# Moving the pass for far sampling points of a fused attention, deformable-convolution and MLP kernel into the main schedule, with its tables in DRAM

## The chip, the cores and the metric

The kernel runs on one core of one Trainium2 chip. The metric is the device time of one execution in microseconds, as the median of several runs. A trace of one profiled execution of the kernel before is at hand as well.

## The reference, cut to what matters

Four images of 64 x 64 tokens with 256 channels pass through self-attention over the 4096 tokens of an image (queries and keys of 32 channels, a residual scaled by a learned factor). Then comes a block of three parts: LayerNorm; a deformable 3 x 3 convolution (DCNv3) with residual; LayerNorm, an MLP (256 to 1024 to 256, GELU) and residual. All is float32.

The change concerns the deformable convolution. Per token, a small branch computes 16 groups x 9 points = 144 sampling points, each with an offset in x, an offset in y and a softmax weight:

```python
px = loc_x * Win - 0.5            # token + point of the 3x3 grid + offset
py = loc_y * Hin - 0.5
x0 = jnp.floor(px); y0 = jnp.floor(py)
lx = px - x0;       ly = py - y0
val = gather(y0, x0) * ((1 - ly) * (1 - lx))[..., None] + gather(y0, x0 + 1) * ((1 - ly) * lx)[..., None] \
    + gather(y0 + 1, x0) * (ly * (1 - lx))[..., None] + gather(y0 + 1, x0 + 1) * (ly * lx)[..., None]
out = jnp.einsum('nhwgpc,nhwgp->nhwgc', val, mask).reshape(N, H, W, C)
```
`gather` reads the 16 channels of the point's group from the projected image, zero outside the padded image. The sampled sum is then multiplied with a 256 x 256 output matrix.

## The kernel before, in words

**Tiling.** The 16384 tokens are cut into 64 units (4 images x 16, `NU` = 16 per image) of 256 tokens: four image rows, two tokens on each of the 128 partitions. For each unit there are stages, written as dictionaries of small named steps:

- `project` and attention, for the next image's keys and for this unit's tokens; attention is most of TensorE's work.
- `front`: residual, first LayerNorm, input projection, whose result goes to the DRAM image `xp`.
- `plan`: the depthwise branch, the heads that give offsets and mask (tile `om`, 2 x 432 numbers per partition, stored to DRAM as `omd` in `weigh`, L676), the bilinear weights as `hat`, and from those the weights `wn` of a 5 x 5 window.
- `sample`: VectorE multiplies five shifted rows `win` with `wn` (`times`, L785) and adds them up (`plus`, L793; `across`); the sums go to DRAM as `spd`.
- `back`: output projection, second LayerNorm and MLP, through `finish` (L818 to 901); its last step `end` (L885) adds the MLP's result `pmlp` to `x1b`, and SyncE stores it to the output (L912).

**Order.** `whole()` collects the steps of all units, gives each the time `slot * T + WHEN[stage][step]` (T = 60, table `WHEN`), sorts them and emits them in that order, under a manual schedule for TensorE, VectorE, ScalarE and GpSimd. A unit with number s has attention in slot s, `front` in s + 1, `plan` in s + 2, `sample` and `back` in s + 3. Plain DMAs are issued by SyncE's queue in an order of the framework's own.

**Far points.** The 5 x 5 window holds every point whose offsets lie within 1. For others, `am` = min(1 − |x|, 1 − |y|) (`nearer`, L642) is negative; their weight is set to zero (`near`, L681), and `count` (L654 to 661) adds up their number per partition and unit in `cnt`. So the sum in `spd` lacks them, and the tokens after attention, to which the convolution's result is added, are kept in DRAM as `x1d`.

**After the last unit.** The main program calls `whole(False)` (L955). Then:

1. A test over all attention sums and mask sums (L957 to 975), whose last steps are `plow` on TensorE (L970) and three small VectorE operations (L972 to 975). A loop with 0 or 1 rounds (L976) does everything again in a general form, `whole(True)`, if a value is out of range.
2. Tables of indices, ten of them, made by GpSimd's iota (L994) and a VectorE cast (L996), one after the other through one buffer.
3. `cnt` is added up (L1015), the largest over partitions found (L1017 to 1021), and loaded as the number of rounds (L1022).
4. The loop of rounds (L1042 to 1161). A round takes one far point on every partition: it picks the last unit with one (L1045 to 1053), gathers the whole row of `omd` (indirect DMA on GpSimd, L1025), recomputes `am`, finds the point, and picks its x, y, mask, group and row with one-hot multiplies and sums (L1083, L1084). Then it gathers the four corner pixels (`s_px`), adds them to the token's gathered row of `spd`, runs `finish(x1, sp, "fx", 1)` for that one token per partition, and scatters the result to the output (L1030).

Of the kernel before, what the change touches and what calls it, by code (L numbers as in the profile page):

```python
# [8 lines left out]
F32 = mybir.dt.float32  # L9
# [7 lines left out]
def tile_attention_dcnv3_block(  # L17
# [21 lines left out]
    nc = tc.nc  # L39
# [68 lines left out]
    raw = const.tile([P, C // P, 2, CQ], F32, name="raw_qk")  # L108
# [80 lines left out]
    omd = dram.tile([B * NU * P, 2 * NOM], F32, name="omd")  # L189
    x1d_ = x1d.rearrange("(u q p) c -> u p q c", q=2, p=P)  # L190
    spd_ = spd.rearrange("(u q p) c -> u p q c", q=2, p=P)
    omd_ = omd.rearrange("(u p) m -> u p m", p=P)

# [68 lines left out]
    def transposed(src, name, n=2, pool=None, tag="m"):  # L262

        pt = (pool or ps).tile([P, C // P, 256], F32, tag=tag, name=f"pt_{name}")
        for k in range(C // P):
# [59 lines left out]
            "narrowed0": 84.81, "narrowed1": 89.91, "end": 93.7,  # L325
        },
# [224 lines left out]
    def plan(b, u, wns, general):  # L551
# [89 lines left out]
        def nearer():  # L641
            st["am"] = am = p1.tile([P, 2, S], F32, tag="am", name=f"am_{n}")  # L642
            nc.vector.tensor_tensor(
                am, st["hat"][:, 1, :, 0, :], st["hat"][:, 1, :, 1, :], ALU.min
            )

# [269 lines left out]

    def whole(general):
# [29 lines left out]
        if not general:  # L947
            steps += [(3.5 * i - 55.0, len(steps) + i, fn) for i, fn in enumerate(loads)]
# [5 lines left out]
    whole(False)  # L954
# [5 lines left out]
    safe = p1.tile([P, B * NU * 2], F32, tag="am", name="safe")  # L960
    flat = rall.rearrange("p u i -> p (u i)")
    nc.vector.tensor_scalar(safe, flat, 1e9, None, ALU.is_le)
    nc.vector.scalar_tensor_tensor(safe, flat, 1e-15, safe, ALU.is_ge, ALU.mult)
    for t, op, bound in ((least, ALU.is_ge, 1e-15), (most_, ALU.is_le, 1e15)):
        t = t.rearrange("p i g -> p (i g)")
        nc.vector.scalar_tensor_tensor(safe[:, : 2 * G], t, bound, safe[:, : 2 * G], op, ALU.mult)
    low = gx.tile([P, 1], F32, name="low")
    nc.vector.tensor_reduce(low, safe, AX.X, ALU.min)
    plow = ps.tile([1, P], F32, tag="m", name="plow")
    nc.tensor.matmul(plow, lhsT=low, rhs=ident, start=True, stop=True)  # L970
    again = gx.tile([1, 1], F32, name="again")
    nc.vector.tensor_reduce(again, plow, AX.X, ALU.min)  # L972
    nc.vector.tensor_scalar(again, again, -1.0, 1.0, ALU.mult, ALU.add)
    again_i = gx.tile([1, 1], I32, name="again_i")
    nc.vector.tensor_copy(again_i, again)
    with tc.For_i(0, nc.values_load(again_i[0:1, 0:1], min_val=0, max_val=1), 1):  # L976
        whole(True)
    main.close()


    fx = ctx.enter_context(tc.tile_pool(name="fx", bufs=1))
    UN = B * NU
    FAR = float(4 * max(H, W))
    BIG = 4096.0

    def table(shape, pattern, base, name, halves=False, step=0, cm=0):

        size = 1
        for d in shape:
            size *= d  # L990
        ti = fx.tile([P, size], I32, tag="ti", name=f"{name}_i")
        for r in range(2 if halves else 1):
            rows = slice(r * W, (r + 1) * W) if halves else slice(0, P)
            nc.gpsimd.iota(ti[rows], pattern=pattern, base=base + r * step, channel_multiplier=cm)  # L994
        tf = fx.tile([P, size], F32, name=name)
        nc.vector.tensor_copy(tf, ti)  # L996
        return tf

    part = table([1], [[0, 1]], 0, "part", cm=1)
    uid1 = table([UN], [[1, UN]], 1, "uid1")  # L1000
    h0 = table([UN], [[0, B], [4, NU]], 0, "h0")
    rb = table([UN], [[H + 4, B], [0, NU]], 0, "rb")
    sid1 = table([2 * S], [[1, 2 * S]], 1, "sid1")
    gid = table([2 * S], [[0, 2 * KP], [1, G]], 0, "gid")
    iid = table([2 * S], [[1, 2], [0, S]], 0, "iid")
    g16 = table([G], [[1, G]], 0, "g16")

    bx = table([2, 3, 3 * G], [[0, 2], [1, 3], [0, 3 * G]], -1, "bx", halves=True, cm=1)
    by = table([6, 3, G], [[0, 6], [1, 3], [0, G]], -1, "by", halves=True, step=1)
    nc.vector.tensor_scalar(by[:, S:], by[:, S:], 2.0, None, ALU.add)  # L1010

    ptr = fx.tile([P, 1], F32, name="ptr")
    nc.vector.memset(ptr, BIG)
    tot = fx.tile([P, 1], F32, name="tot")
    nc.vector.tensor_reduce(tot, cnt, AX.X, ALU.add)  # L1015
    ptot = ps.tile([1, P], F32, tag="m", name="ptot")
    nc.tensor.matmul(ptot, lhsT=tot, rhs=ident, start=True, stop=True)  # L1017
    most = fx.tile([1, 1], F32, name="most")
    nc.vector.tensor_reduce(most, ptot, AX.X, ALU.max)
    most_i = fx.tile([1, 1], I32, name="most_i")  # L1020
    nc.vector.tensor_copy(most_i, most)
    rounds = nc.values_load(most_i[0:1, 0:1], min_val=0, max_val=UN * 2 * S)  # L1022

    def gather(dst, src, idx):
        nc.gpsimd.indirect_dma_start(  # L1025
            out=dst, out_offset=None, in_=src, in_offset=bass.IndirectOffsetOnAxis(ap=idx, axis=0)
        )

    def scatter(dst, idx, src):
        nc.gpsimd.indirect_dma_start(  # L1030
            out=dst, out_offset=bass.IndirectOffsetOnAxis(ap=idx, axis=0), in_=src, in_offset=None
        )

    def integer(src, name, n=1):
        t = fx.tile([P, n], I32, tag=f"int_{name}", name=f"int_{name}")
        nc.vector.tensor_copy(t, src)
        return t

    def small(name, n=1):
        return fx.tile([P, n], F32, tag=f"s_{name}", name=f"s_{name}")  # L1040

    with tc.For_i(0, rounds, 1):  # L1042

        cu = small("cu", UN)
        nc.vector.scalar_tensor_tensor(cu, cnt, 0.0, uid1, ALU.is_gt, ALU.mult)  # L1045
        u1 = small("u1")
        nc.vector.tensor_reduce(u1, cu, AX.X, ALU.max)
        sel = small("sel", UN)
        nc.vector.tensor_scalar(sel, uid1, u1, None, ALU.is_equal)
        uu = small("uu")  # L1050
        nc.vector.tensor_scalar(uu, u1, 1.0, 0.0, ALU.subtract, ALU.max)
        at_om = small("at_om")
        nc.vector.scalar_tensor_tensor(at_om, uu, float(P), part, ALU.mult, ALU.add)
        om = fx.tile([P, 2 * NOM], F32, tag="f_om", name="f_om")
        gather(om, omd, integer(at_om, "om"))
        om = om.rearrange("p (i m) -> p i m", i=2)


        av = fx.tile([P, 2, 2 * S], F32, tag="f_av", name="f_av")
        ab = fx.tile([P, 2, 2 * S], F32, tag="f_ab", name="f_ab")  # L1060
        nc.vector.tensor_scalar(av, om[:, :, : 2 * S], -1.0, 0.0, ALU.mult, ALU.max)
        nc.vector.tensor_scalar(ab, om[:, :, : 2 * S], 0.0, None, ALU.max)
        nc.vector.scalar_tensor_tensor(  # L1063
            av, av, 1.0, ab, ALU.subtract, ALU.subtract, reverse0=True
        )
        am = fx.tile([P, 2, S], F32, tag="f_am", name="f_am")
        nc.vector.tensor_tensor(am, av[:, :, :S], av[:, :, S:], ALU.min)  # L1067
        am = am.rearrange("p i s -> p (i s)")
        nc.vector.scalar_tensor_tensor(am, am, 0.0, sid1, ALU.is_lt, ALU.mult)
        nc.vector.scalar_tensor_tensor(am, am, ptr, am, ALU.is_lt, ALU.mult)  # L1070
        s1 = small("s1")
        nc.vector.tensor_reduce(s1, am, AX.X, ALU.max)
        oh = fx.tile([P, 2 * S], F32, tag="f_oh", name="f_oh")
        nc.vector.tensor_scalar(oh, sid1, s1, None, ALU.is_equal)

        def pick(src, mask, dst, three=None):
            t = fx.tile([P, 2 * S], F32, tag="f_pick", name="f_pick")
            n = mask.shape[1]
            tv, mv = t[:, :n], mask
            if three:  # L1080
                tv = tv.rearrange("p (i s) -> p i s", i=2)
                mv = mask.rearrange("p (i s) -> p i s", i=2)
            nc.vector.tensor_mul(tv, src, mv)  # L1083
            nc.vector.tensor_reduce(dst, t[:, :n], AX.X, ALU.add)  # L1084

        xy, m, g, ti, rbs, h0s = small("xy", 2), small("m"), small("g"), small("ti"), small("rbs"), small("h0s")
        at = fx.tile([P, 2, S], F32, tag="f_at", name="f_at")
        nc.vector.tensor_add(at, om[:, :, :S], bx.rearrange("p (i s) -> p i s", i=2))
        pick(at, oh, xy[:, 0:1], True)
        at = fx.tile([P, 2, S], F32, tag="f_at", name="f_at2")  # L1090
        nc.vector.tensor_add(at, om[:, :, S : 2 * S], by.rearrange("p (i s) -> p i s", i=2))
        pick(at, oh, xy[:, 1:2], True)
        pick(om[:, :, 2 * S :], oh, m, True)
        nc.vector.scalar_tensor_tensor(m, u1, 0.0, m, ALU.is_gt, ALU.mult)
# [99 lines left out]
```

## Time and profile before

| what | us |
|---|---|
| median of 3 runs | 3935.21 (3930.83 to 3937.36) |
| the profiled execution | 3932.3 |
| its span in the trace | 3930.1 |
| TensorE busy in the span | 3788.7 (96%) |
| VectorE busy | 3418.2 (87%) |
| ScalarE busy | 1995.8 (51%) |
| GpSimd busy | 310.8 (8%) |
| mean granted TensorE clock | 0.981 of full |

The page shows TensorE (PE) nearly always busy: attention's `acc` matmuls alone (L471) are 1902.1 us. VectorE (DVE) is second; its largest groups are the window multiplies (L785, 936.6 us) and adds (L793, 759.0 us), of 1481 and 1482 ns each.

How to read the views: in the page's slices each digit is the busy share of a fortieth of the span (98 us), in tenths, and PEclk the clock granted to TensorE. A row of a timeline has the start, the duration, the engine, the line of the kernel, the operation with the tile it writes and those it reads, its shape, and in brackets the idle time of that engine ahead of it with what ended it. A row of a group of one line has min/median/max ns and the first and last start. `PEldq`, `DVEq`, `SPq` and so on are instructions of an engine's own sequencer, such as branches and DMA issues.

### The profile page before, as it was taken

What the parts mean: (1) busy time and instruction counts of PE and PEld (TensorE: products, weight loads), DVE (VectorE), ACT (ScalarE), POOL (GpSimd) and SP (SyncE); (2) the same over time, 40 slices, a digit from 0 to 9 for tenths busy, and PEclk for the clock granted to TensorE, in tenths of its full rate; (3) what the DMA queues carried; (4) which work ended last, traced back from release to release, by engine and by line L of the source; (5) the groups of instructions that cost most, each with busy time, mean ns of one, the idle gap of its engine ahead of it and who ended that gap; (6) DMA issues with size and microseconds to landing.
All of it is one profiled execution on the core that took longest, in us unless ns stands there. A gap on an engine that the chain in (4) does not pass through costs nothing. (4 is left out here: it accounts for less than half of the span.)

```text
span 3930.1 us, 56100 instructions
## 1 busy us (share of the span) xinstructions
PE 3788.7 (96%) x20284; PEld 3124.9 (80%) x20284; DVE 3418.2 (87%) x6160; ACT 1995.8 (51%) x3986; POOL 310.8 (8%) x437
## 2 busy tenths in 40 slices
PE   8999999999999999999999999999999999999853
PEld 7878888888888888888888888888888888888642
DVE  1499899999999999999989999999999999999992
ACT  4555555545555555555555554555555555555321
POOL 1000000000000000000000000000000000000001
PEclk9999999999999999999999999999999999999966
DMA  5334334335344333434443433433543334333320
GB/s 146 97 104 112 92 103 116 92 100 159 99 119 115 97 103 107 105 98 136 123 111 104 116 92 100 115 101 99 150 106 102 100 102 104 91 99 94 97 58 15
DMA packets 342769, 410.64 MB, mean 104 GB/s; under 512 B 136017, under 2 KB 292753, under 8 KB 342481
## 3 DMA queue, kind: packets, MB, share of 16 engines
q1 hardware_dynamic: 332544, 399.84, 38.2%
q10 hardware_dynamic: 8512, 3.43, 0.4%
q8 instruction: 162, 2.65, 0.3%
q0 software_dynamic: 1424, 3.69, 0.3%
q14 instruction: 127, 1.03, 0.1%
HBM read 277.00 MB, written 129.83 MB: 104 GB/s over the span
## 5 line engine op out<-in xcount | busy, mean ns | idle before, releaser
L471 PE MATMUL acc<-V,ex 128*128 128x257 f32 x8192 | 1902.1, 382 | 0.2 <-DVE x L500 0.2
L471 PEld LDWEIGHTS acc<-V,ex 128*128 128x128 f32 x8192 | 1528.7, 190 | 260.0 <-issue 65.4
L785 DVE TENSOR_TENSOR pw<-win,wn 128x1280 f32<-128x1280 f32 x640 | 936.6, 1481 | 7.0 <-ACT gT L870 0.5
L793 DVE TENSOR_TENSOR pw<-pw,pw 128x1280 f32<-128x1280 f32 x512 | 759.0, 1482 | 0.2
L459 ACT ACTIVATE ex<-e 128x512 f32<-128x512 f32 x1024 | 527.4, 600 | 214.6 <-PE e L446 207.1
L862 PE MATMUL ph<-hT_b,f1w 128*128 128x256 f32 x2048 | 496.3, 387 | 3.2 <-ACT hT_b L247 2.7
L870 ACT ACTIVATE gT<-ph,f1b 128x256 f32<-128x256 f32 x512 | 241.1, 471 | 475.2 <-PE ph L862 475.2
L879 PE MATMUL pmlp<-f2w,gT 128*128 128x256 f32 x2048 | 468.0, 382 | 0.0
L862 PEld LDWEIGHTS ph<-hT_b,f1w 128*128 128x128 f32 x2048 | 385.1, 192 | 80.6 <-issue 18.6
L572 DVE SCALAR_TENSOR_TENSOR cv<-hs,dw,cv 128x256 f32<-128x256 f32 x1024 | 436.4, 477 | 6.4 <-ACT cv L568 6.4
L879 PEld LDWEIGHTS pmlp<-f2w,gT 128*128 128x128 f32 x2048 | 385.9, 192 | 55.1 <-issue 5.3
L239 ACT ACTIVATE xn_p<-pc,nm_p,rstd_p 128x256 f32<-128x256 f32 x128 | 65.2, 560 | 615.9 <-DVE nm_p L231 615.9
L446 PE MATMUL e<-qs,kT 32*128 32x256 f32 x4096 | 305.5, 403 | 0.7 <-ACT ex L459 0.7
L446 PEld LDWEIGHTS e<-qs,kT 32*128 32x128 f32 x4096 | 192.0, 184 | 86.1 <-issue 53.0
L257 ACT ACT_TABLE_LOAD x192 | 246.3, 1283 | 2.6
L225 POOL TENSOR_SCALAR rstd_p<-mv_p 128x2 f32<-128x2 f32 x64 | 81.6, 1274 | 1562.2 <-DVE mv_p L223 1562.2
L606 PE MATMUL po<-om_w,ge 128*128 128x432 f32 x512 | 199.9, 534 | 1.3 <-ACT ge L599 1.3
L694 DVE TENSOR_TENSOR pr<-hat 128x1296 f32<-128x1296 f32 x128 | 192.5, 1504 | 6.7
L537 DVE TENSOR_TENSOR xq<-pp,inb 128x512 f32<-128x512 f32 x64 | 44.2, 691 | 138.8 <-PE pp L530 138.8
L606 PEld LDWEIGHTS po<-om_w,ge 128*128 128x128 f32 x512 | 98.9, 194 | 73.3 <-issue 57.4
L225 POOL TENSOR_SCALAR rstd_b<-mv_b 128x2 f32<-128x2 f32 x64 | 21.2, 331 | 1369.2 <-DVE mv_b L223 1348.3
L378 PE MATMUL pv<-wv_s,xT 128*128 128x256 f32 x512 | 126.9, 391 | 2.3 <-DVE V L386 2.3
(239 smaller groups left out, 3685.2 us busy)
## 6 DMA issues: line engine op xcount, KB each, us to landing
win<-xp SPq DMA_DIRECT2D x536, 320.0 KB, 4.6
omd<-om SPq DMA_DIRECT2D x64, 432.0 KB, 2.8
hs<-himg SPq DMA_DIRECT2D x128, 160.0 KB, 3.2
xs<-in_x_dram SPq DMA_DIRECT2D x64, 256.0 KB, 2.8
x<-in_x_dram SPq DMA_DIRECT2D x64, 256.0 KB, 3.0
himg<-hT_f SPq DMA_DIRECT2D x128, 128.0 KB, 2.9
xp<-xq SPq DMA_DIRECT2D x128, 128.0 KB, 2.4
x1d<-x SPq DMA_DIRECT2D x64, 256.0 KB, 3.2
```

The source lines that it names most:

```text
L257: nc.scalar.activation(idle, minus_half[:, 0:1], func)
L446: nc.tensor.matmul(es[r][:, jj, :], lhsT=self.kT[2 * g + jj][rows4(r), :], rhs=self.qs[rows4(r), :], start=True, stop=not self.general,)
L459: nc.scalar.activation(ex, self.es[r], AF.Exp)
L471: nc.tensor.matmul(self.acc[i], lhsT=ex[:, jj, i * P : (i + 1) * P], rhs=V[t // 2][:, t % 2, :], start=(g == 0 and r == 0 and jj == 0), st ...
L572: nc.vector.scalar_tensor_tensor(acc, src, dw[:, k, j : j + 1], acc, ALU.mult, ALU.add)
L606: nc.tensor.matmul(st["po", i], lhsT=st["ge"][:, k, i * P : (i + 1) * P], rhs=om_w[:, k, :], start=(k == 0), stop=(k == 1),)
L694: nc.vector.tensor_mul(pr.rearrange("p a b c d g -> p a b (c d g)"), hat[:, :, i, 1, :].unsqueeze(1).to_broadcast([P, 3, 3, S]), hat[:, :, ...
L785: nc.vector.tensor_mul(st[r].rearrange("p d (g c) -> p (d g) c", c=GC), src.rearrange("p d (g c) -> p (d g) c", c=GC), wns[b, u][:, i, r] ...
L793: nc.vector.tensor_add(st[0], st[0], st[r])
L862: nc.tensor.matmul(ph[:, :m], lhsT=f1w[:, k, c * P : (c + 1) * P], rhs=st["hT"][:, k, :m], start=(k == 0), stop=(k == 1),)
L870: nc.scalar.activation(st["gT"][:, c, :m], st["ph", c][:, :m], AF.Gelu, bias=f1b[:, c : c + 1])
L879: nc.tensor.matmul(po, lhsT=st["gT"][:, c, i * P : (i + 1) * P], rhs=f2w[:, c, :], start=(c == 0), stop=(c == NH - 1),)
```

## The change

- At the start of the program, tables by point (`tab_s`: group, x and y of the grid, which of the two tokens), by unit (`tab_u`) and of running numbers (`tab_n`) are made with iota and cast and stored to DRAM by GpSimd DMAs; small ones (`where`, `rev`, `g16`) stay in SBUF. `raw_qk` moves to another pool.
- `nearer` stores `am` to DRAM as `amd` in every unit (SyncE DMA of 128 x 288 floats).
- The body of a round becomes `far_round(units)`. Rather than `omd`'s row it gathers the row of `amd`, finds the point there, and then gathers three single numbers of `omd` and the point's and the unit's row of the tables, so the picks are gone. The rest of the round (four corners, sum, `finish`, scatter) has the same arithmetic.
- One such pass over units 0 to 60 is put into the main schedule, in slot 66 with times of its own in `WHEN` ("far": from −84 to +50.89). The range test and a test whether any far point is left ("checks") are put there too.
- After `whole(False)` only one number is loaded; one outer loop of 0 or 1 rounds holds the general loop and the loop of further far rounds over all 64 units.

On VectorE, the emitted order puts the pass's first steps behind the shift of `plan`'s norm of unit 62 and its last step just ahead of the last unit's final addition; the test stands among the window multiplies of unit 63. On GpSimd, the twelve gathers and the scatter to `spd` stand between the norm of `plan` of unit 62 and that of `back` of unit 61.

```diff
...
     omd = dram.tile([B * NU * P, 2 * NOM], F32, name="omd")
+    amd = dram.tile([B * NU * P, 2 * S], F32, name="amd")
...
+    tab_s = dram.tile([2 * S, 4], F32, name="tab_s")
+    tab_u = dram.tile([UN, 2], F32, name="tab_u")
+    tab_n = dram.tile([2 * S], F32, name="tab_n")
...
+        "far": {
+            "unit": -84, "point": -80, "left": -77, "rows": -76, "pixels": -74, "summed": -66, "turn": 34.5,
...
+            "narrowed0": 50.29, "end": 50.89,
+        },
+        "checks": {
+            "range": 12.0, "left": 12.1, "largest": 12.2,
+        },
...
                 am, st["hat"][:, 1, :, 0, :], st["hat"][:, 1, :, 1, :], ALU.min
             )
+            nc.sync.dma_start(amd_[b * NU + u], am.rearrange("p i s -> p (i s)"))
...
+    def far_round(units):
...
+        def unit():
+            t = wide(units, f"f_u_{n}")
+            V_.scalar_tensor_tensor(t, cnt[:, :units], 0.0, rev[:, :units], ALU.is_gt, ALU.mult)
+            V_.tensor_reduce(col("u1"), t, AX.X, ALU.max)
...
+            gather(st["am"], amd[: units * P], integer(0, col("row")))
+            gather(col("by_u", 2), tab_u, integer(1, col("uu")))
+            st["sid"] = wide(2 * S, f"f_sid_{n}")
+            nc.sync.dma_start(st["sid"], tab_n.partition_broadcast(P))
...
+            gather(col("by_s", 4), tab_s, integer(2, col("s0")))
+            for k, name in enumerate(("x", "y", "m")):
+                if k:
+                    V_.tensor_scalar(col("at"), col("at"), float(S), None, ALU.add)
+                gather(col(name), omd[: units * P].rearrange("r (m o) -> (r m) o", o=1), integer(8 + k, col("at")))
...
+        if not general:
+            put(B * NU + 2, "far", far_round(B * NU - 3))
+            put(B * NU + 2, "checks", checks)
...
-    with tc.For_i(0, nc.values_load(again_i[0:1, 0:1], min_val=0, max_val=1), 1):
-        whole(True)
...
-    rounds = nc.values_load(most_i[0:1, 0:1], min_val=0, max_val=UN * 2 * S)
...
-    with tc.For_i(0, rounds, 1):
...
+    whole(False)
+    res = todo["res"]
+    with tc.For_i(0, nc.values_load(res[0:1, 1:2], min_val=0, max_val=1), 1):
+        with tc.For_i(0, nc.values_load(res[0:1, 0:1], min_val=0, max_val=1), 1):
+            whole(True)
+            nc.vector.memset(ptr, BIG)
+        nc.vector.tensor_reduce(tot[:, 0:1], cnt, AX.X, ALU.add)
+        res = largest_of(1, "rounds")
+        with tc.For_i(0, nc.values_load(res[0:1, 0:1], min_val=0, max_val=UN * 2 * S), 1):
+            for step in far_round(UN).values():
+                step()
```

## The prediction

> **What bounds the kernel now.** I read the page's slices first, then the windows at the end of the span, then the timeline of the last 75 us, and last the groups of single lines.
>
> ```profile
> PE   8999999999999999999999999999999999999853
> DVE  1499899999999999999989999999999999999992
> PEclk9999999999999999999999999999999999999966
> ```
> For some 3690 us TensorE is full. Only the last two or three slices (98 us each) are not, and the change is almost all there.
>
> ```profile
> 3500.00:3560.00 60.00, 60.00 (x322) 49.46 (x321) 56.59 (x97) 31.68 (x63) 4.40 (x6) 1.00 0.42 107
> 3740.00:3760.00 20.00, 14.38 (x52) 11.15 (x52) 19.79 (x34) 8.04 (x17) 1.17 (x2) 0.73 0.28 66
> 3800.00:3820.00 20.00, 16.74 (x65) 13.66 (x65) 19.76 (x20) 6.03 (x11) 0.00 (x0) 0.87 0.13 34
> 3840.00:3860.00 20.00, 17.58 (x69) 14.07 (x69) 1.81 (x5) 4.81 (x10) 0.00 (x0) 0.84 0.02 7
> 3860.00:3880.00 20.00, 0.59 (x2) 0.09 (x2) 4.26 (x22) 0.00 (x0) 4.71 (x13) 0.58 0.04 13
> ```
> The numbers after the window's length are busy us of PE, PEld, DVE, ACT and POOL. One unit of the steady state (first row) is PE-bound, with 3.4 us of DVE to spare. Once attention has ended (about 3690) the last units drain, and there DVE is the bound (19.8 of 20 us). From 3840 the last MLP is PE's alone, and after 3860 nearly nothing runs.
>
> ```profile
> 3857.96 0.69 DVE L885 TENSOR_TENSOR x1b<-x1b,pmlp 128x512 f32<-128x512 f32 x1 [17.31 <-PE pmlp L879]
> 3865.40 0.22 DVE L1015 TENSOR_REDUCE tot<-cnt 128x1 f32<-128x64 f32 x1
> 3869.11 0.59 PE L1017 MATMUL ptot<-ident,tot 128*1 128x128 f32 x2 [10.88 <-issue]
> 3875.99 0.24 DVE L1010 TENSOR_SCALAR by<-by 128x144 f32<-128x144 f32 x1
> 3878.38 1.10 POOL L1025 DMA_INDIRECT f_om<-omd,int_om  x1 [2.77 <-DVE int_om L1036]
> 3882.47 0.46 DVE L1061 TENSOR_SCALAR f_av<-f_om 128x576 f32<-128x576 f32 x1 [4.37 <-DMA f_om<-omd,int_om]
> 3896.21 0.94 POOL L1025 DMA_INDIRECT s_px<-xp,int_at  x1 [0.79 <-DVE s_at_x L1124]
> 3904.33 0.69 PE L267 MATMUL pt_s_fx<-ident,f_sp 128*128 128x128 f32 x2 [34.63 <-DVE f_sp L1150]
> 3922.35 0.42 DVE L885 TENSOR_TENSOR f_x<-f_x,pmlp_fx 128x256 f32<-128x256 f32 x1 [11.32 <-PE pmlp_fx L879]
> 3923.07 1.08 POOL L1030 DMA_INDIRECT out_dram<-f_x,int_tok  x1 [13.32 <-DVE f_x L885]
> ```
> The last unit is added up at 3857.96. What follows is serial: the skipped general loop (to 3865.4, on PE to 3869.1), the tables (to 3876.2), one far round of gathers, picks and an MLP (to 3924.2), and leaving the program at 3930.1. Removable tail: 3930.1 − (3857.96 + 0.69) = 71.5 us.
>
> **Does one pass suffice?** Computing the offsets from the reference's inputs gives six points beyond 1, the largest 1.091 and the two nearest 1.0012 and 1.0019, in units 12, 27, 38, 47, 50 and 60, on six partitions; the next below is 0.990. That fits the trace, where the round ran once. One pass clears a point on every partition, and the pass of the change takes units 0 to 60. In units 61 to 63 the largest are 0.911, 0.905 and 0.940. So no point is left over, and the new outer loop is skipped.
>
> **Start and steady state.** About ten small table copies go to DVE at the start; their order puts them among the first V copies, where DVE idles 2.3 to 3.7 us at a time for PE (25 to 48 us): 0, at most +1. Each unit gets one more SP transfer, the `am` store (147 KB). Its source is ready at 3010.72 in one unit, the `omd` store ahead of it issues at 3010.49 for 0.41, and the next SP issue is a `win` at 3027.69. So it lies in a 16.8 us hole, with DMA at 40%: 0. Without that cover it would be 0.4 us by 64 units, 26 us.
>
> **The pass in the drain.** The instruction order puts the pass's DVE work after `nm_p` of unit 62 and up to the last unit, where DVE is the bound, so each op counts. Pitches are from the tail: 0.49 for a 128x288 op, 0.24 for 64 wide, 0.15 to 0.18 for a column.
> - unit 8 ops 1.5; point 3 x 0.49 + 12 x 0.18 = 3.65; left 1.05; pixels 35 x 0.157 = 5.5; summed 4 small and two 256-wide, 2.1. Sum 13.8.
> - Waits for gathers. Undisturbed, `f_om` came 4.1 us after its issue. `am` is a third as large; I take 3.8, with two DVE ops (2.25 us) between: 1.5 uncovered. The four columns and the four corners are issued at a pitch of 1.25 and have 5 and more ops of the last units in between: 1.0. Sum 2.5 undisturbed; with what the next part adds, 7.0 (0 to 15).
> - Against that, DVE's idles for `po` (0.54) and `pout` (1.22) in the drain take pass work in: −1.7.
> - The final test, 10 DVE ops: 1.65, plus 1.0 for its PE step and 0.4 behind it: +3.0. The range test is in before's trace too, but earlier ops of it lie in idle time (3791 to 3794.5), so I credit only the last three.
> - The pass's projection and MLP for one token per partition. DVE adds, statistics and residual 2.75 (1.1 of it waiting for POOL's rstd), the final add 0.4, and a wait for its `pmlp` that PE finishes between the last two units: 1.4 (0 to 4). PE's own 13 us fit in its idle time (5 to 9 us free of every 20). A warmer PE ahead of the last projection gives −1.9.
>
> Sum +24.8 (14 to 36): the last unit's add moves from 3857.96 to about 3882.8.
>
> **Weighing a rule.** The Trainium skill ("SBUF — State Buffer", section "SBUF: two separate sides") says that GpSimd writes the descriptors of DMAs issued from its queue, and that a DVE instruction in a two-port mode, or with two SBUF inputs, locks it out of their common ports until it ends. That speaks against this change: in the tail the gathers ran beside an idle or lightly loaded DVE, now they run beside 1.48 us multiplies with two inputs. The rows:
>
> ```profile
> L225 POOL TENSOR_SCALAR rstd_p<-mv_p x64: 217/1291/1293, 161.0 to 3769.0; 128x2 f32<-128x2 f32 x64
> ...
> 3837.59 0.22 POOL L225 TENSOR_SCALAR rstd_b<-mv_b 128x2 f32<-128x2 f32 x1 [39.97 <-DVE mv_b L223]
> ```
> The same small POOL op takes 0.22 us beside an idle DVE and 1.29 beside a long one, so the lock is visible. For the gathers themselves the nearest rows are those of the round: 0.94 to 1.10, even over short two-input DVE ops. By these rows the twelve gathers and the scatter cost POOL 13 us and DVE the 2.5 above. By the rule each gather can wait out one multiply (1.48): the `am` wait +1.5, four columns in a row +5.9, the four corners partly covered +2, some 9 us more. What follows the gathers on DVE in the new order are mostly two-input multiplies and adds of 1.48 (L842, L850), so I can't keep the row alone; but a gather meets a multiply at any point of it, and waits half of one on average. I take half, +4.5, and keep 0 and 9 for the range.
>
> **Behind the last unit.**
>
> ```profile
> L976 PEldq COMPARE_BRANCH  x3: 97/308/3996, 3860.2 to 3868.7; - x3
> ...
> L1190 POOLq DRAIN  x3: 44/104/2775, 3926.4 to 3929.8; - x3
> ```
> One loop skip is left. In before it took the load (0.8), then a jump of 4.0 on PE and the engines' semaphores, PE out of it 8.5 us after 3860.5. The same jump now ends the program, with about 1 us for the closing barrier, POOL's drain (2.8) beside it: 9.5 after PE's last matmul, which is where the add starts (7 to 13). Tables, both loads, the picks and the cold MLP are gone from here.
>
> So span = 3882.8 + 9.5 = 3892.3, against 3930.1: −37.8. The profiled execution was 3932.3, 2.2 over its span: 3894.5. The median of the runs (3935.2) is 2.9 over the profiled one: 3897.4, so I give **3897**.
>
> **Rivals.**
> - The lock decides: the full 9 us gives 3902; if the four columns and `am` each sit out several multiplies (4 us each rather than 1), +19 instead of +4.5, 3912. For: the 1.29 row. Against: the undisturbed 0.95 beside column ops.
> - The gathers run free and the cover is better: −4.5, and DVE's remaining idle (8 us in 3820 to 3840) takes in the pass's MLP ops, −4, with a short exit, −3: 3886. Against: most of that idle lies behind the last DVE sampling op, when the pass is done.
> - Slower than before: the `am` store blocks SP. It waits in SP's queue for a DVE result, with `win`, `hs` and `himg` behind it. If `am` came late against the next `win`, every unit would lose; at (3935.2 − 3897)/64 = 0.60 us per unit the gain is gone, at 1 us it is 3961. Against: `am` ends 17.0 us ahead of that `win`.
> - It doesn't do what it says: a leftover point opens the outer loop. Count, matmul, loads and the inner skip about 10 us each, and a round with cold PE 40 to 45: 3897 + 60 = 3957. It needs an offset over 1 in the last three units, where the largest is 0.940.
>
> **How the numbers follow.** Forecast 0.57 (3889 to 3904), lock above its half 0.20 (3902 to 3914), free gathers and more cover 0.18 (3878 to 3889), SP 0.03, leftover 0.02. Eight in ten lie within 3881 to 3913. A measurement of this kernel can tell about 0.2% (7.9 us) from no change; faster by more needs under 3927: 0.95, within 0.02, slower 0.03.
>
> **What would show it.** In the new profile: one `L1197` skip and no far ops behind the last `x1b` add; that add near 3883; the DVE windows from 3740 to 3860 near 20 of 20, with about 25 us more work and waits in them; gathers between 1 and 2.4 us on POOL, and some 7 us of DVE waits on them; the steady window still 60.00 PE. Wrong it would be with DVE waits on gathers over 12 us in all or none, an exit over 13 us, or a window of the steady state longer than before.

## The result and the profile after

The changed kernel takes 3889.76 us (median of 4 runs, 3888.52 to 3892.32); the kernel before, in the same sessions, 3935.51 (4 runs, 3930.83 to 3937.36). The ratio is 0.9886, with a 95% interval of 0.9869 to 0.9903: faster by 1.1%. The profiled execution took 3889.96, its span is 3888.1, and the mean granted clock 0.988.

The page's slices of the changed kernel answer to those shown of before:

```profile
PE   8999999999999999999999999999999999999946
DVE  2399989989989989989989989999999999999995
PEclk9999999999999999999999999999999999999977
```
Only two slices at the end are still thin. The windows, with the same columns as before (length, then busy us of PE, PEld, DVE, ACT and POOL):

```profile
3500.00:3560.00 60.00, 60.00 (x323) 49.69 (x322) 56.59 (x99) 30.91 (x62) 4.20 (x6) 1.00 0.43 112
3720.00:3740.00 20.00, 6.20 (x14) 2.72 (x13) 15.19 (x42) 4.18 (x7) 10.15 (x8) 0.78 0.33 88
3740.00:3760.00 20.00, 4.68 (x11) 3.00 (x11) 18.80 (x70) 4.18 (x11) 8.64 (x9) 0.59 0.19 64
3840.00:3860.00 20.00, 13.32 (x62) 11.22 (x62) 11.28 (x17) 5.45 (x14) 2.13 (x4) 0.83 0.06 20
3860.00:3880.00 20.00, 17.92 (x68) 14.35 (x68) 1.38 (x2) 5.38 (x12) 0.00 (x0) 0.83 0.01 2
```
The steady state is unchanged: in the first row PE is full and DVE as busy as before (56.59). A unit takes 55.70 us there in both kernels, and the norm of unit 61's `plan` comes 3501.61 us after that of unit 0 in the kernel before and 3501.62 us in the changed one (rows under am_x4). The pass's gathers and sums stand at 3722 to 3754: POOL, at 8% over the whole span, is busy 8.6 to 10.2 of 20 us, mostly with the gathers, and DVE waits for gathers there (15.19 of 20 us busy). The window from 3860 to 3880, nearly empty before, is now the last unit's MLP. Behind that there is only the exit.

From the timeline of the changed kernel (start, duration, engine, line, operation, idle before):

```profile
3720.23 0.69 DVE L942 TENSOR_TENSOR x1b<-x1b,pmlp 128x512 f32<-128x512 f32 x1 [1.05 <-PE pmlp L936]
...
3724.28 1.49 DVE L850 TENSOR_TENSOR pw<-pw,pw 128x1280 f32<-128x1280 f32 x1
3724.64 2.10 POOL L985 DMA_INDIRECT f_am_f<-amd,ints  x1 [4.60 <-DVE x L579]
3729.16 0.46 DVE L1031 SCALAR_TENSOR_TENSOR f_am_f<-f_am_f,f_sid_f 128x288 f32<-128x288 f32 x1 [3.40 <-DMA f_am_f<-amd,ints]
3731.76 0.94 POOL L985 DMA_INDIRECT scal<-tab_s,ints  x1 [3.73 <-DVE ints L1010]
3732.74 1.49 DVE L842 TENSOR_TENSOR pw<-win,wn 128x1280 f32<-128x1280 f32 x1
3733.01 2.05 POOL L985 DMA_INDIRECT scal<-omd,ints  x1 [0.30 <-DVE ints L1010]
...
3740.37 0.16 DVE L1061 SCALAR_TENSOR_TENSOR scal<-scal 128x1 f32<-128x1 f32 x1 [0.79 <-DMA scal<-omd,ints]
3754.80 0.68 DVE L901 TENSOR_TENSOR x1b<-x1b,pout 128x512 f32<-128x512 f32 x1
...
3852.24 0.42 DVE L942 TENSOR_TENSOR f_x_f<-f_x_f,pmlp_f 128x256 f32<-128x256 f32 x1 [3.30 <-PE pmlp_f L936]
3854.27 1.99 PE L895 MATMUL pout<-ow,sT 128*128 128x256 f32 x8 [0.68 <-ACT sT L889]
...
3878.92 0.69 DVE L942 TENSOR_TENSOR x1b<-x1b,pmlp 128x512 f32<-128x512 f32 x1 [17.61 <-PE pmlp L936]
```
A gather that is issued beside a multiply or add of 1.49 ends 0.8 to 1.0 us after that operation does: L850 ends at 3725.77 and the `am` gather at 3726.74; L842 ends at 3734.23 and the next gather at 3735.06. Column operations (one number a partition, 0.15 us each) don't hold it: the gather at 3731.76, beside six of them, took 0.94. DVE waits for gathers twice, 3.40 and 0.79 us.

**The ledger.** The last unit's add moved from 3857.96 to 3878.92, and what follows it (from its end) shrank from 71.5 to 3888.1 − 3879.61 = 8.5 us. To take the chance of the start out, I count from the first plan's norm on POOL (161.00 in before, 162.72 after) to the last unit's add: 3696.96 before, 3716.20 after. So the drain costs 19.24, the start 1.72, and the tail gives 63.0: together −42.0, the difference of the spans.

### The profile page after: what moved, and what is told of

It is laid out like the page before. It is cut to its first block, busy times and chain, and to the rows that moved or that the text cites. A ratio compares the mean times of both kernels' runs of the same rounds, so it can differ in the third digit from the quotient of the medians.

```text
span 3888.1 us, 56223 instructions
## 1 busy us (share of the span) xinstructions
PE 3783.9 (97%) x20284; PEld 3120.9 (80%) x20284; DVE 3413.4 (88%) x6157; ACT 1996.0 (51%) x3986; POOL 320.0 (8%) x445
## 3 DMA queue, kind: packets, MB, share of 16 engines
q8 instruction: 162, 2.65, 0.3%
q14 instruction: 126, 1.03, 0.1%
## 4 chain that ended last, share of the span: by engine, by line
PE 95%; DVE 4%; DMA 1%; issue 0%; ACT 0%; POOL 0%; SPq 0%; POOLq 0%; ACTq 0%; DVEq 0%
PE acc L527 46%; PE ph L919 11%; PE pmlp L936 11%; PE e L502 7%; PE po L662 5%; PE pv L434 3%; PE pout L895 3%; PE pp L586 3%; PE pkq L413 1%; DVE pw L842 1%; PE pc L638 1%; PE pt_s L311 1%; PE pt_p L311 1%; PE pt_f L311 1%; PE pt_b L311 1%; PE pt_x L311 1%
## 5 line engine op out<-in xcount | busy, mean ns | idle before, releaser
L842 DVE TENSOR_TENSOR pw<-win,wn 128x1280 f32<-128x1280 f32 x640 | 937.1, 1482 | 7.0 <-ACT gT L927 0.4
L850 DVE TENSOR_TENSOR pw<-pw,pw 128x1280 f32<-128x1280 f32 x512 | 759.2, 1483 | 0.2
```

What stands on the lines that cost most here:

```text
L842: nc.vector.tensor_mul(st[r].rearrange("p d (g c) -> p (d g) c", c=GC), src.rearrange("p d (g c) -> p (d g) c", c=GC), wns[b, u][:, i, r] ...
L850: nc.vector.tensor_add(st[0], st[0], st[r])
```

## Experiments

All start from the changed kernel. "Count" is the distance just described, 3716.20 in the changed kernel, read from one profiled execution; its start differs by chance from kernel to kernel, so that count shows smaller effects than the median. "Short" is the same with a later start: the addition of unit 60's `pmlp` (L942), just ahead of the pass's first step, at 3720.23 in the changed kernel. Where the drain is the same, both counts agree to 0.2 us (changed kernel, tables_apart and am_x4; no_pass and pass_at_end). In the kernel before they are 3696.96 and 139.12. In early_steps and early_all the pass begins ahead of that addition, so they have no short count.

Why two counts: VectorE's wait for TensorE ahead of that addition differs although the kernels are alike up to there. It is 1.05 in the changed kernel, but for instance

```profile
3720.29 0.69 DVE L942 TENSOR_TENSOR x1b<-x1b,pmlp 128x512 f32<-128x512 f32 x1 [2.43 <-PE pmlp L936]
```
in gathers_beside, whose edit comes after the last unit. The clock granted in the 9 us before it was 0.65 in the changed kernel and 0.57 in gathers_beside, and the last 16 matmuls for `pmlp` took 4.60 and 5.98 us.

| kernel | median us (range) | ratio to before (95%) | span | count | short |
|---|---|---|---|---|---|
| changed kernel | 3889.76 (3888.52 to 3892.32) | 0.9886 (0.9869 to 0.9903) | 3888.1 | 3716.20 | 158.69 |
| no_pass | 3872.62 (3872.11 to 3875.52) | 0.9847 (0.9831 to 0.9863) | 3870.1 | 3699.31 | 141.77 |
| pass_at_end | 3924.82 (3922.94 to 3927.49) | 0.9976 (0.9968 to 0.9985) | 3920.8 | 3699.42 | 141.69 |
| later_steps | 3889.18 (3888.03 to 3889.70) | 0.9887 (0.9871 to 0.9904) | 3886.0 | 3715.25 | 156.57 |
| finish_early | 3896.10 (3894.76 to 3898.44) | 0.9906 (0.9890 to 0.9923) | 3892.8 | 3723.22 | 164.52 |
| checks_late | 3888.56 (3885.81 to 3890.45) | 0.9883 (0.9866 to 0.9899) | 3886.8 | 3714.27 | 156.56 |
| tables_apart | 3889.36 (3888.38 to 3891.13) | 0.9887 (0.9870 to 0.9903) | 3886.7 | 3716.23 | 158.72 |
| combined | 3891.73 (3891.03 to 3893.86) | 0.9893 (0.9877 to 0.9910) | 3888.9 | 3718.25 | 160.78 |
| early_steps | 3891.51 (3891.19 to 3896.24) | 0.9896 (0.9879 to 0.9912) | 3889.4 | 3717.71 | – |
| early_all | 3893.23 (3888.97 to 3894.78) | 0.9894 (0.9877 to 0.9910) | 3891.5 | 3717.53 | – |
| late_both | 3885.81 (3885.03 to 3887.43) | 0.9878 (0.9861 to 0.9894) | 3884.5 | 3714.79 | 156.81 |
| am_x4 | 3890.96 (3889.79 to 3891.39) | 0.9889 (0.9873 to 0.9906) | 3889.7 | 3716.43 | 158.87 |

**no_pass: what the pass costs where it stands.** The pass is left out, so the six far points are missing from the output.

```diff
-            put(B * NU + 2, "far", far_round(B * NU - 3))
...
-        nc.vector.scalar_tensor_tensor(tot[:, 1:2], tot[:, 1:2], 0.0, tot[:, 0:1], ALU.is_gt, ALU.max)
+        nc.vector.scalar_tensor_tensor(tot[:, 1:2], tot[:, 1:2], 1e6, tot[:, 0:1], ALU.is_gt, ALU.max)
```


> The pass is not issued and leftovers are not counted, so the six far points are left out of the output; tables, am stores and the final test stay. Theory (VectorE bounds the drain, so the pass is paid there): the 15 us by which the last plan's norm came later plus about 6 us of the pass's MLP chain go, a span of 3867 to 3872 against 3888.1. Rival (the pass lies beside other work and the moved tail is all there is): a span above 3880.

Measured: span 3870.1, the theory's side. The count falls by 16.9 us. So the pass is paid for in the drain: 15.4 of it lies ahead of the last plan's norm (3607.61 on the same count, 3622.99 in the changed kernel), and only 1.5 comes behind that, where I had expected 6. The timeline of this kernel shows why so little:

```profile
3834.92 3.78 PE L895 MATMUL pout<-ow,sT 128*128 128x256 f32 x8 [0.68 <-ACT sT L889]
3838.74 0.69 DVE L901 TENSOR_TENSOR x1b<-x1b,pout 128x512 f32<-128x512 f32 x1 [5.45 <-PE pout L895]
3861.41 0.69 DVE L942 TENSOR_TENSOR x1b<-x1b,pmlp 128x512 f32<-128x512 f32 x1 [17.76 <-PE pmlp L936]
```
Without the pass's MLP ahead of it TensorE is cold (a granted clock of 0.50 from 3834 to 3839.5), the last projection takes 3.78 us, and DVE waits 5.45 for it. In the changed kernel the clock is 1.00 from 3852 to 3857, the projection takes 1.99 and the wait is 3.31: 2.1 us come back. Against the kernel before, this one has a count higher by 2.35: the price of the final test, since the `am` stores add nothing (am_x4).

**pass_at_end: the move or the tables?**

```diff
-            put(B * NU + 2, "far", far_round(B * NU - 3))
```


> The pass is left to the loop behind the test; everything else as in the changed kernel. Theory (the gain is the move, and the tables only save some 15 us of the tail): last unit's add near 3862, then two loop tests of about 10 us, a serial round of some 52 us, exit: about 3930 (3920 to 3942), near the kernel before. Rival (the tables are the gain): about 3900.

Measured: 3924.82, with a span of 3920.8. The move is the gain; all else of the change gives 0.24%. Its timeline:

```profile
3861.01 0.69 DVE L942 TENSOR_TENSOR x1b<-x1b,pmlp 128x512 f32<-128x512 f32 x1 [18.01 <-PE pmlp L936]
...
3867.48 0.22 DVE L1200 TENSOR_REDUCE tot<-cnt 128x1 f32<-128x64 f32 x1 [5.79 <-issue]
...
3869.84 0.23 DVE L1017 SCALAR_TENSOR_TENSOR f_u_f<-cnt,rev 128x64 f32<-128x64 f32 x1 [1.00 <-DVE res_rounds L1186]
...
3911.77 1.08 POOL L990 DMA_INDIRECT out_dram<-f_x_f,ints  x1 [12.32 <-DVE f_x_f L942]
```
Two loop tests take 5.8 us, the count 2.4, the round 43.0, the exit 8.0: 59.1, against 71.5 in before. So the tables, and the test moved with them, save 12.4 us of a serial tail and cost 2.5 on the count (3699.42 against 3696.96).

**later_steps: are the waits for gathers pure loss?**

```diff
-            "unit": -84, "point": -80, "left": -77, "rows": -76, "pixels": -74, "summed": -66, "turn": 34.5,
+            "unit": -84, "point": -76, "left": -74.7, "rows": -74.6, "pixels": -70.3, "summed": -62, "turn": 34.5,
```


> The same pass with its point, left, pixel and sum steps put later, so that VectorE has 4.8 us of other work behind the am gather and 6.9 us behind the four column gathers. Theory (VectorE-bound, waits of 3.40 and 0.79 us are pure loss): about 4 us less, a span near 3884. Rival (port lock: with more multiplies beside them the gathers stretch and the waits stay): within 1.5 us of 3888.

Measured: count −0.95, span 3886.0, of which 1.1 is a luckier start. The median is the same. The gathers didn't stretch more (2.10 at most), and DVE's waits for them fell from 4.19 to 0.72, so the rival's reason is out; but the gain is well under the theory's 4 us. DVE's waits in this kernel:

```profile
3720.31 0.69 DVE L942 TENSOR_TENSOR x1b<-x1b,pmlp 128x512 f32<-128x512 f32 x1 [2.22 <-PE pmlp L936]
3729.38 0.46 DVE L1031 SCALAR_TENSOR_TENSOR f_am_f<-f_am_f,f_sid_f 128x288 f32<-128x288 f32 x1 [0.72 <-DMA f_am_f<-amd,ints]
3750.97 0.69 DVE L901 TENSOR_TENSOR x1b<-x1b,pout 128x512 f32<-128x512 f32 x1 [1.49 <-PE pout L895]
```
The first one, 2.22 against 1.05, lies ahead of the pass, where the two kernels are alike: it is the chance described above (a clock of 0.58 in the 9 us before; combined, with the same later steps, waits 1.01 there), and it hides 1.2 us of the gain. From there on, on the short count, the gain is 2.1. DVE did not wait for unit 61's `pout` in the changed kernel (3754.80) and waits 1.49 here, as in late_both and combined (1.48). 3.47 us of waits for gathers went and 1.49 us for TensorE came, which leaves 2.0. A wait removed is partly a wait moved.

**finish_early: the pass's MLP in TensorE's idle time.** All its steps from "turn" to "end":

```diff
-            ... "turn": 34.5,
+            ... "turn": -24.10,
...
-            "narrowed0": 50.29, "end": 50.89,
+            "narrowed0": -8.31, "end": -7.71,
```


> The pass's projection and MLP put 58.6 us of the schedule earlier, ahead of the last plan's heads, where TensorE is half idle. Theory (at the end the chain runs through the pass's MLP, 6.5 + 3.5 us on TensorE, of which VectorE covers all but 3.6): 3 to 4 us less, a span near 3884.5. Rival (it only delays the last unit's heads in TensorE's queue, and VectorE waits there instead): 3887 to 3891.

Measured: slower than the changed kernel by 7.0 on the count and by 5.8 on the short one, worse than the rival said. The last plan's heads stand behind the pass's MLP in TensorE's queue, and DVE waits for them, for the hats made from them, and for the MLP:

```profile
3800.95 0.61 DVE L671 TENSOR_TENSOR om<-po,om_b 128x432 f32<-128x432 f32 x1 [1.72 <-PE po L662]
3802.40 0.61 DVE L671 TENSOR_TENSOR om<-po,om_b 128x432 f32<-128x432 f32 x1 [0.84 <-PE po L662]
3806.60 0.76 DVE L693 SCALAR_TENSOR_TENSOR hat<-hat 128x576 f32<-128x576 f32 x1 [0.99 <-ACT hat L689]
3812.68 0.42 DVE L942 TENSOR_TENSOR f_x_f<-f_x_f,pmlp_f 128x256 f32<-128x256 f32 x1 [4.45 <-PE pmlp_f L936]
```
That is 8.0 us, where the changed kernel has 0.94 for these heads and 3.30 for the MLP. At the end the warm clock is lost too: DVE waits 5.45 for the last projection. Of these two places the later one, where the changed kernel has the MLP, is the better.

**checks_late: the price of the final test.**

```diff
-            "range": 12.0, "left": 12.1, "largest": 12.2,
+            "range": 64.0, "left": 64.1, "largest": 64.6,
```


> The ten operations of the final test moved behind the last unit's norm, where VectorE waits 17 us for the last MLP. Theory (VectorE-bound where they stand): their 2.8 us go, less 0.6 for the test's matmuls between those of the last MLP: a span near 3886. Rival (the drain is not bound by VectorE there, or the late number delays the exit): 3888 or more.

Measured: count −1.93, short count −2.1, span 3886.8 with a start 0.7 later than the changed kernel's. As the theory said (2.2): DVE does the ten operations inside the wait for the last MLP (of which 11.79 remain unbroken, of 17.61), and the exit is no later: 9.1 us from the add to the end, 9.2 in the changed kernel. The median lies 1.2 below, which the runs alone can't tell from none.

**tables_apart: the start.**

```diff
-    tab = p1.tile([P, 2 * S], F32, tag="mk", name="tab_c")
+    tab = p1.tile([P, 2 * S], F32, tag="om", name="tab_c")
```


> The third table is built in a buffer of its own rather than waiting for the store of the second (4.43 us of VectorE's idle at 35 to 40 us). Theory (that wait cools TensorE and makes the first unit 1.73 us late): about 1.5 us less, a span near 3886.5, first plan's norm no later than in the kernel before. Rival (the lag is the chance of the start's loads): within 0.5 us, lag anywhere from 0 to 2.

Measured: count the same (3716.23), median 0.4 lower. The first norm came at 161.36, in the kernels with the old table buffer it came at anything from 160.69 (finish_early) to 165.18 (early_all), and at 161.91 in combined, which has the new one. The rival holds: the start's lag is chance, and the 4.43 us wait there is covered.

**combined: do the four add?** The four edits above together.

> All four together: later steps, early MLP, late test, own table buffer. Theory (the four terms add): 4 + 3.5 + 2.2 + 1.5, a span near 3877 and a median near 3879. Rival (each only uncovers the next wait): 3883 to 3886.

Measured: median 3891.73, count +2.05, short count +2.1, so neither the theory nor the rival. The early MLP spoils it. The sum of the four is −0.95 + 7.02 − 1.93 + 0.03 = +4.2 on the count and −2.12 + 5.83 − 2.13 + 0.03 = +1.6 on the short one; with the chance in single waits that late_both shows, whether they add stays open.

**gathers_beside: the port by itself.** At the end of the program, for each kind of VectorE work (`op`; the lines that set up the tiles are left out here):

```diff
+            for q in range(4):
+                gather(dst[:, q * GC : (q + 1) * GC], src, idx[:, k : k + 1])
+            for _ in range(8 if op else 0):
+                op()
```


> Behind the last unit, five groups of four gathers of 16 floats per partition, each group beside a VectorE stream of another kind: none, two-input multiplies of SBUF tiles, one-input multiplies, multiplies with one operand in PSUM, and sums over the free dimension. Theory (a two-input VectorE operation holds the port until it ends): 0.94 us per gather alone and in the PSUM and sum groups, about 1.5 to 2.4 beside two-input multiplies. Rival (the stretch seen is DMA load of the drain): 0.94 in all groups. Open: the one-input group.

Measured in one execution (3930.71 us with the added work, which says nothing of the change); some gathers of each group in its timeline:

```profile
3877.66 0.95 POOL L985 DMA_INDIRECT probe_alone<-xp,probe_i  x1 [0.30 <-issue]
...
3881.88 1.94 POOL L985 DMA_INDIRECT probe_two<-xp,probe_i  x1 [2.01 <-DVE probe_i L1216]
3884.12 1.23 POOL L985 DMA_INDIRECT probe_two<-xp,probe_i  x1 [0.30 <-issue]
...
3885.66 1.70 POOL L985 DMA_INDIRECT probe_two<-xp,probe_i  x1 [0.30 <-issue]
...
3894.62 1.44 POOL L985 DMA_INDIRECT probe_one<-xp,probe_i  x1 [5.74 <-DVE probe_i L1216]
...
3903.19 0.94 POOL L985 DMA_INDIRECT probe_psum<-xp,probe_i  x1 [1.96 <-DVE probe_i L1216]
...
3910.36 0.94 POOL L985 DMA_INDIRECT probe_stats<-xp,probe_i  x1 [2.48 <-issue]
```
0.95 alone; 1.94, 1.23, 1.70 and 1.22 beside two-input multiplies of SBUF tiles; 0.94 beside multiplies with an operand in PSUM, and beside sums. DMA load is out as a cause: the DMA engines' share was 0.05 while the gathers ran alone, 0.02 around the first of the stretched ones (3881.5 to 3884.4) and 0.03 around the one-input group (3894 to 3901). Not all of it runs on an empty machine: the first group lies beside TensorE's last MLP, and the last unit's add and store (3884.45 and 3885.16) fall among the two-input multiplies. The open group is settled too: one-input multiplies of an SBUF tile (0.86 us each) stretch a gather to 1.42 to 1.44.

**early_steps: DVE's slack ahead of the drain.**

```diff
-            "unit": -84, "point": -80, "left": -77, "rows": -76, "pixels": -74, "summed": -66, "turn": 34.5,
+            "unit": -162, "point": -156.5, "left": -156.4, "rows": -87, "pixels": -88, "summed": -78, "turn": 34.5,
```


> The pass's unit, point and left steps (6.0 us of VectorE and its wait for the am gather) put into the last attention slot, where VectorE has 3.4 us to spare in 60 and TensorE is full; pixels and sum a little earlier than in the changed kernel. Counted from the first plan's norm to the last unit's add, which takes the chance of the start out (3716.2 us in the changed kernel). Theory (VectorE's slack in the TensorE-bound stretch takes the work in): 3 to 4 us less, 3712.5. Rival (as with the later steps, what is taken away comes back as waits for TensorE): within 1 us of 3716.

Measured: count +1.5, so both were wrong. From the timeline of this kernel, in the last attention slot:

```profile
3658.09 0.46 DVE L1031 SCALAR_TENSOR_TENSOR f_am_f<-f_am_f,f_sid_f 128x288 f32<-128x288 f32 x1 [3.19 <-DMA f_am_f<-amd,ints]
3658.63 0.60 ACT L515 ACTIVATE ex<-e 128x512 f32<-128x512 f32 x1 [2.22 <-DVE f_am_f L1031]
3668.99 1.21 PE L638 MATMUL pc<-ident,cv 128*128 128x128 f32 x4 [7.41 <-DVE cv L628]
```
Attention's exponentials wait for the pass's `am` tile, which lies in their ring of buffers; DVE's taps `cv` come late, and TensorE waits 7.41 us for them. Attention's last matmul came at 3700.6, against 3691.1. An average slack of 3.4 us in a unit did not take in 6 us in one piece with a wait of 3.2 in it.

**early_all: everything earlier.** The edits of early_steps and checks_late, and the pass's MLP behind unit 62's heads:

```diff
-            ... "turn": 34.5,
+            ... "turn": -74.00,
...
-            "narrowed0": 50.29, "end": 50.89,
+            "narrowed0": -58.21, "end": -40.0,
```

> Early steps, the late test, and the pass's projection and MLP placed behind the heads of the last but one plan, 108.5 us of the schedule earlier, with its final add 49 us later than its matmuls. Theory (TensorE has 10 us idle in 20 there, and no heads stand behind it): 3.5 + 1.9 + 1.5 less than 3716.2, some 3709. Rival (unit 61's projection behind it in TensorE's queue comes later and VectorE waits for that): 3713 or more.

Measured: count +1.3, the rival's side. DVE waits 3.08 for unit 61's projection, and 5.45 for the last one, which is cold again (3.78 us on TensorE).

**late_both: the two that helped.** The edits of later_steps and checks_late.

> Later steps and late test together, the MLP left where the changed kernel has it. Theory (the two gains of 0.95 and 1.93 us, counted from the first plan's norm, add): 3713.3 us on that count, a median near 3887. Rival (one cover, used twice): 3714.3 or more.

Measured: count −1.41, where 2.9 was the sum, and short count −1.9, where 4.25 was: the rival's number. But its reason, one cover used twice, is not what the trace shows. Up to the final test this kernel has the steps of later_steps, and there it lost 2.6 us against it by unit 62's `pout`, in waits for TensorE (unit 61's `pmlp`: 2.46 against 1.15, and the heads behind it). In later_steps and here:

```profile
3786.26 0.69 DVE L942 TENSOR_TENSOR x1b<-x1b,pmlp 128x512 f32<-128x512 f32 x1 [1.15 <-PE pmlp L936]
...
3786.28 0.69 DVE L942 TENSOR_TENSOR x1b<-x1b,pmlp 128x512 f32<-128x512 f32 x1 [2.46 <-PE pmlp L936]
```
The 16 matmuls for that `pmlp` took 6.01 us rather than 4.70, in 6 us with a granted clock of 0.50 rather than 0.72. So chance took what the second gain brought, and whether the two add stays open. Its median, 3885.81, is the lowest of the versions with the pass, and all its runs lie under all of the changed kernel's (3885.03 to 3887.43 against 3888.52 to 3892.32). The two intervals of the ratio to before overlap, and 1.7 of its span's 3.6 us are a luckier start; so 1.4 to 1.9 us are shown by the trace, and the runs agree in sign.

**am_x4: the cover of the `am` store.**

```diff
             nc.sync.dma_start(amd_[b * NU + u], am.rearrange("p i s -> p (i s)"))
+            nc.sync.dma_start(amd_[b * NU + u], am.rearrange("p i s -> p (i s)"))
...
```


> Each unit stores its am four times over to the same place: three more transfers of 147 KB on SyncE's queue per unit. Theory (they lie in the queue's hole of 16.8 us): 0, the steady unit stays at 60.00 us and the median within 3 us of 3890. Rival (each issue costs its 0.4 us): 3 x 0.4 x 64 = 77 us more.

Measured: median 3890.96, count +0.2. Unit 61's norm in the kernel before, the changed kernel and this one, whose first norms are at 161.00, 162.72 and 163.77:

```profile
3662.61 1.29 POOL L225 TENSOR_SCALAR rstd_p<-mv_p 128x2 f32<-128x2 f32 x1 [23.21 <-DVE mv_p L223]
...
3664.34 1.29 POOL L269 TENSOR_SCALAR rstd_p<-mv_p 128x2 f32<-128x2 f32 x1 [23.20 <-DVE mv_p L267]
...
3665.36 1.29 POOL L269 TENSOR_SCALAR rstd_p<-mv_p 128x2 f32<-128x2 f32 x1 [23.20 <-DVE mv_p L267]
```
That is 3501.61, 3501.62 and 3501.59 us: 61 stores, or four times as many, cost nothing. Part of SyncE's queue in one unit of this kernel:

```profile
3013.77 0.40 SPq L702 DMA_DIRECT2D amd<-am  x1
...
3019.97 0.32 SPq L705 DMA_DIRECT2D amd<-am  x1
3030.47 2.56 SPq L826 DMA_DIRECT2D win<-xp  x4
```
Four stores end at 3020.3, and 10 us of the hole are still free. The rival of a blocked SyncE queue is out by a wide margin.

## Why the prediction was right, point by point

- **One pass suffices, the outer loop is skipped**: yes; after the last add there are only the skip of L1197 and the exit.
- **Start 0 to +1**: +1.72 in the profiled execution, but by chance (tables_apart).
- **`am` stores 0**: shown, by the norms under am_x4. The sign I named, 60.00 of PE, could not have shown a longer unit: it is a window of 60 us in which TensorE is full, and a unit takes 55.70.
- **The pass's operations 13.8**: 12.95 by the timeline (unit 1.37, point 3.58, left 1.03, pixels 4.95, summed 2.02).
- **Waits for gathers 7.0**: 4.19. This is the term most off. The mechanism was right: five of the thirteen gathers and scatters were clearly held, 4.9 us of POOL time in all, four of them until the end of the DVE operation in progress and the fifth (1.90 from 3747.36) until the end of a second, short one. But I had let every gather wait half a multiply. The stretch of the four gathers for single numbers and the table row lay beside DVE work except for 0.79, and the corners were covered in full. And later_steps shows that 3.5 us less of these waits are worth 2 us, since a wait for TensorE grows.
- **The rule against the rows**: the Trainium skill ("SBUF — State Buffer", section "SBUF: two separate sides") is narrower than I put it, for two SBUF inputs count only against a GpSimd operation that reads SBUF. A gather here reads its indices from an SBUF tile (`ints`, `probe_i`), and two-input multiplies did hold it (1.22 to 1.94 in gathers_beside). In time, the rows alone gave 2.5 us of DVE waits, half of the rule 7.0 and the full rule some 11.5; measured were 4.19, of which later_steps took 3.47 away with gathers still held.
- **Idle taken in −1.7**: −1.8 to −2.2 (12.95 + 4.19 − 15.4 against no_pass, and − 14.97 against before, on the count).
- **Final test +3.0**: +2.35, and 1.93 come back when it is moved.
- **The pass's MLP +2.65 in all**: +1.5. From the last plan's norm to the end of L857, its work costs next to nothing (63.2 us, against 63.1 in no_pass and 62.8 in pass_at_end), so the 2.75 put for its adds and statistics were covered. Then the wait for its `pmlp`, 3.30 rather than 1.4, and its last addition stand ahead of the last unit's sum `sp` (L859) on VectorE, not only ahead of its final addition, and hold the last projection; the warm clock gave back 2.1 where 1.9 was put. No run moved that addition alone.
- **Exit 9.5 from the add's start**: 9.2, though not quite by the route I gave. The sequencers' instructions behind the last unit, of the loop and of the program's end:

```profile
L1197 PEldq COMPARE_BRANCH  x3: 97/197/3752, 3875.5 to 3884.4; - x3
...
L1235 POOLq DRAIN  x3: 40/103/3428, 3883.7 to 3887.8; - x3
```
  TensorE's long jump (3.75 us, from 3879.2, right behind its last matmul) is there as in before, where it took 4.0. But TensorE was out of the loop 1.5 us after it, not 4.5, and the end was then set by POOL's drain (3.4 us from 3883.7), which I had put beside the rest, and SyncE (3887.0).
- **From span to median**: I added 2.9 for the gap between before's profiled execution and its median. The changed kernel's profiled execution is 0.2 above its median. The gap of one execution is chance, and should have been left at nothing in the middle and put in the range.

The error of 7.6 us (3897.4 against 3889.8) is made of: drain −5.5 (24.75 against 19.24), start +1.7, exit and frame (from span to execution) −0.7, gap −3.1. All terms of the drain but the idle were put too high, the waits for gathers most. There is luck in how near it came: without the 1.7 us of chance at the start, the profiled execution would have been at some 3888, below the 3889 to 3904 that I thought most likely and among the numbers of the rival with free gathers.

Of the rivals, the full lock, the blocked queue and the leftover point are out. "Gathers run free and the cover is better" was half right: they don't run free, but the cover is better (waits for gathers 2.8 under mine, the MLP 1.15 under).

## What to carry to other kernels

A serial tail of 60 us could be moved under the draining units for the price of its operations on the engine that bounds the drain, here 17 us. What can go wrong is in the queues: what stands behind the moved step on each engine can cost more than the step (the MLP put 58.6 us earlier in the schedule made it 6 to 7 us slower). A wait that is seen in the trace is worth only what is left when the next wait has grown. To see effects of 1 or 2 us, take the distance between two fixed events rather than the total, put the first one right ahead of the change, and look for waits that differ where the kernels are alike: here one such wait moved by 1.4 us with the granted clock. And the best place found for a test whose result is used at the very end was inside the last unavoidable wait.

## What the runs showed of the hardware that was not expected

- A gather from GpSimd's queue (0.94 us) is held also by one-input VectorE multiplies from SBUF to SBUF (1.42), a group that I had left open. They take 0.86 us for the tile that two-input ones take 1.50 for; whether they are in the two-port mode of the rule, no run here shows. It was not held beside multiplies with an operand in PSUM (0.72 us each) nor beside sums over the free dimension (1.5 us each), as the theory had it.
- It was held for the operation in progress, not for the stream: beside back-to-back multiplies of 1.5 us it took 1.22 to 1.94, never several of them. In all traces here no gather took over 2.14.
- The start varies by 4.5 us between kernels whose start is the same (first norm at 160.69 to 165.18), more than most of the effects studied here.
- In the drain the granted clock differs between kernels with the same steps (0.57 to 0.65 in the same 9 us), and with it one wait of VectorE (1.01 to 2.43).
